# Split of the next image and close of the image before emitted in turn, in half-size pieces, with all planes made by GpSimd

## The chip, the cores and the metric

The kernel runs on one core of one Trainium2 chip. The metric is the device time of one execution in microseconds. A core has five engines that each run their own instructions in order: PE (matrix products), DVE (vector), ACT (scalar, activations), POOL (GpSimd) and SP (here it only issues DMAs). All work is in float32, but for some rows of the scan.

## What is computed

The input is x of shape (4, 96, 128, 128). Each of the four images goes through a state-space block (a projection, a depthwise convolution, four scans over the image, a layer norm, a projection back, added to x) and then through an attention block. The change lies in the second, cut here to what matters. `n` is the image after the first block, normalised; `sc`, `nc`, `res` are scalars of the input.

```
x   = n - mean(n)                                    # per image
x1  = relu(x);  x2 = x - x1                          # the split: positive and negative half
x1n = sqrt(pos/total) * layer_norm(x1 + avg1 * (x1 == 0))
x2n = sqrt(neg/total) * layer_norm(x2 + avg2 * (x1 > 0))
e   = 0.5 * (nc1*x1n + nc2*x2n) + res * x
x1, x2 = sc1*x1 + x1n, sc2*x2 + x2n

key, value = conv3x3(x1, aw1), conv3x3(x1, aw3)      # 96 -> 96 channels each
query, c2  = conv3x3(x2, aw2), conv3x3(x2, w_conv2)
attn = softmax(key . query over 3x3 patches / sqrt(96*9))    # a 96 x 96 x 3 x 3 kernel per image
o    = conv3x3(value, attn)
out  = x + e + w_full . [norm(o), x1 * norm(c2)] + b_full    # the close
```

## The kernel before, in words

**Stages.** Up to 2300 us the first block runs for all images. Then come four attentions, one image b after the other. The convolutions of images 1 to 3 are made from products of *planes*: a row of 128 pixels is cut into 32 groups of four, and six planes of 32 columns are linear combinations of neighbouring pixels. The planes of a half-image are made in SBUF, stored to DRAM (`x1p`, `x2p` for the two halves of the split, `vp` for the value) and read back by the attention in strips of 12 rows (`ya`, `yc`). Image 0 uses plain maps for its first convolutions and planes for the last one.

**Per image beside the attention**, a lighter stream of work runs:
- `norm` (`ssm_output`, L924) ends the first block and writes `xnew` to DRAM.
- `split_norm` (L1081) reads `xnew` twice. The first pass counts (L1123 to L1137). Then some forty small operations turn the sums into scales (L1142 to L1203). The second pass (L1222 to L1253) reads pieces of 8 rows (`SN` = 1024 elements per channel). ACT scales a half into PSUM (`bank`, L1243, two instructions of 512), DVE cuts it by the sign into `half` (L1247), and `planes_of` (L1372) makes the planes.
- `planes_of` has two ways. `scaled` (L1408), for the positive half: ACT makes two scaled copies, `x4` (L1411) and `x2` (L1412), and then POOL does ten additions and subtractions (L1420 to L1425 and four at L1390). `at_once` (L1392), for the negative half: DVE does nine operations (L1397 to L1404 and four at L1390) into `plv`. The caller's argument `vector=lambda i, second: second` picks the way. The value planes of the attention use `scaled` too.
- `close` (`attn_output`, L2247) of the image before reads `od`, `c2d` and `xnew` in pieces of 1024. ACT scales twice (L2231, L2236), DVE does four operations with two SBUF inputs (L2232, L2273, L2237, L2238), PE two matmuls per 512 (L2281, L2282), and DVE adds (L2284 for image 0, L2286 for the others). A memset on POOL (L2226) writes the row of ones into each piece of `o` before it is loaded.

**Order.** Each stream is a generator that emits instructions and yields a cost. `co_run` (L291) steps the attention, and for each cost that it yields steps the light stream until as much (times a pace) has been emitted. At the start of the next image the rest is emitted at once (`drain`, L2548). The light stream is a chain: norm, then split of image b+1, then close of image b-1 (L2552 to L2556). `until` (L2430) steps it further if the loads of the next image would read rows whose planes are not yet stored. `Later` (L306) holds pieces of work for a number of ticks. Engines then run in order, mostly by emission: a ready instruction may stand ahead of one that isn't, as at 4750 us, where PE runs products of image 2 between the matmuls of the close of image 0.

**Buffers** that the prediction speaks of: `x4` two, `x2` one, `pl` and `plv` one each, two tiles for the positive half and one for the negative (L1216), three for `xn`, and two banks of PSUM for the whole light stream (`psr`, L2509).

Of the kernel before, what the change touches and what calls it, by code (L numbers as in the profile page):

```python
# [69 lines left out]
def kernel(  # L70
# [273 lines left out]
    def chain(*gens):  # L344
        for g in gens:
            yield from g

# [733 lines left out]
    def split_norm(xnew, x1d, x2d, stats, keep, cnt, ps, side, planes, vector, done):  # L1081


        with ExitStack() as pools:
            p4 = pools.enter_context(tc.tile_pool(name="n4", bufs=3, side=side))
# [35 lines left out]
            p1 = ExitStack()  # L1121
            p2 = p1.enter_context(tc.tile_pool(name="n1", bufs=2, side=side))
# [15 lines left out]
            p1.close()  # L1138
            p2 = pools.enter_context(tc.tile_pool(name="n2", bufs=2, side=side))
            for i in range(3):  # L1140
                piece(i)
            c5 = col("c5", 5)  # L1142
            nc.vector.tensor_reduce(c5, cnt, AX.X, ALU.add)
            pt = bank(ps)[:C, 0:5]
            nc.tensor.matmul(pt, lhsT=mean96, rhs=c5, start=True, stop=True)
            g5 = col("g5", 5)
            nc.vector.tensor_scalar(g5, pt, float(C), None, ALU.mult)

            num, s1, s2 = col("num", 2), col("s1", 2), col("s2", 2)
            for d, at, of in ((num, 0, None), (s1, 1, 3), (s2, 2, 4)):  # L1150
                nc.vector.tensor_copy(d[:, 0:1], g5[:, at : at + 1])
                if of is None:
                    nc.vector.tensor_scalar(
                        d[:, 1:2], g5[:, 0:1], -1.0, TOTAL, ALU.mult, ALU.add
                    )
                else:
                    nc.vector.tensor_sub(d[:, 1:2], g5[:, of : of + 1], g5[:, at : at + 1])
            inv = col("inv", 2)
            nc.vector.reciprocal(inv, num)
            avg, navg = col("avg", 2), col("navg", 2)  # L1160
            nc.vector.tensor_mul(avg, s1, inv)
            nc.vector.tensor_scalar(navg, avg, -1.0, None, ALU.mult)

            var = col("var", 2)
            nc.vector.tensor_mul(var, s1, avg)
            nc.vector.tensor_sub(var, s2, var)
            nc.vector.tensor_scalar(var, var, 1.0 / TOTAL, 0.0, ALU.mult, ALU.max)


            sa = col("a", 2)  # L1170
            rsqrt2 = col("rsqrt2", 2)
            nc.vector.tensor_scalar(rsqrt2, var, LN_EPS, None, ALU.add)
            nc.scalar.activation(rsqrt2, rsqrt2, AF.Sqrt)
            nc.vector.reciprocal(rsqrt2, rsqrt2)
            nc.vector.tensor_scalar(sa, num, 1.0 / TOTAL, None, ALU.mult)
            nc.scalar.activation(sa, sa, AF.Sqrt)
            nc.vector.tensor_mul(sa, sa, rsqrt2)
            kept = col("kept", 9, 3)
            shift = kept[:, 0:2]
            nc.vector.tensor_mul(shift, sa, navg)  # L1180
            scale = kept[:, 2:4]
            nc.vector.tensor_add(scale, sa, scal[:, 0:2])


            rs, rh, half = col("rs", 2), col("rh", 2), col("half", 2)
            nc.vector.tensor_scalar(half, scal[:, 3:5], 0.5, None, ALU.mult)
            nc.vector.tensor_mul(rs, half, sa)
            nc.vector.tensor_mul(rh, half, shift)
            nc.vector.tensor_scalar(rs, rs, res, None, ALU.add)
            up, low = kept[:, 4:6], kept[:, 6:8]  # L1190
            nc.vector.tensor_sub(up[:, 0:1], rs[:, 0:1], rs[:, 1:2])
            nc.vector.tensor_sub(up[:, 1:2], rh[:, 0:1], rh[:, 1:2])
            nc.vector.tensor_copy(low[:, 0:1], rs[:, 1:2])
            nc.vector.tensor_add(low[:, 1:2], rh[:, 1:2], bful)

            for m, s in ((scale, shift), (up[:, 0:1], up[:, 1:2]), (low[:, 0:1], low[:, 1:2])):
                nc.vector.scalar_tensor_tensor(s, m, shift0, s, ALU.mult, ALU.add)
                nc.vector.tensor_scalar(m, m, a, None, ALU.mult)
            nc.vector.tensor_scalar(low[:, 0:1], low[:, 0:1], 1.0, None, ALU.add)
            thr = kept[:, 8:9]  # L1200
            nc.vector.reciprocal(thr, a)
            nc.vector.scalar_tensor_tensor(thr, shift0, -1.0, thr, ALU.mult, ALU.mult)
            keep.update(up=up, low=low, thr=thr, scale=scale, shift=shift)  # L1203

            def stored(i, m, h):
                if planes:
                    def then(pl):
                        store_planes(nc.sync, m, i * RS, RS, pl)
                        done[m is x2d] = (i + 1) * RS

                    return planes_of(later, p2, h, RS, then, vector=vector(i, m is x2d))
                at = (i * RS + 1) * PW
                return lambda: nc.scalar.dma_start(m[:, at : at + RS * PW], h)

            half = [
                [p2.tile([C, RS * PP], F32, name=f"half{j}{k}", bufs=1) for k in range(2 - j)]  # L1216
                for j in range(2)
                if planes
            ]
            for h in sum(half, []):  # L1220
                nc.gpsimd.memset(h.rearrange("p (a b) -> p a b", b=PB)[:, :, TN:PB], 0.0)
            for i in range(NS):  # L1222
                y = ahead.pop(0)
                piece(i + 3)
                for side_, m in ((0, x1d), (1, x2d)):
                    op = ALU.is_le if side_ else ALU.is_gt
                    if planes:
                        h = half[side_][i % len(half[side_])]
                        v, to = (
                            t.rearrange("p (a b) -> p a b", b=b)[:, :, 0:TN]  # L1230
                            for t, b in ((y, TN), (h, PB))
                        )
                        k, parts = TW * R, 2
                    else:
                        h = p2.tile([C, RS * PW], F32, name=f"half{side_}", bufs=4)
                        hv = h.rearrange("p (h w) -> p h w", w=PW)
                        nc.gpsimd.memset(hv[:, :, 0:1], 0.0)
                        v, to = y.rearrange("p (h w) -> p h w", w=W), hv[:, :, 1:PW]
                        k, parts = RS, 1
                    for a in range(0, k * parts, k):  # L1240
                        x, o = v[:, a : a + k], to[:, a : a + k]
                        f = part(ps, C, k, TN) if planes else o
                        nc.scalar.activation(  # L1243
                            f, x, AF.Identity,
                            scale=scale[:, side_ : side_ + 1], bias=shift[:, side_ : side_ + 1],
                        )
                        later(lambda o=o, x=x, f=f, op=op: nc.vector.scalar_tensor_tensor(  # L1247
                            o, x, thr, f, op, ALU.mult
                        ))
                    later(stored(i, m, h), 1 + 3 * side_ * planes)  # L1250
                for _ in range(6 if planes else 1):
                    later.tick()
                    yield 2.5 if planes else 3.5  # L1253
            later.flush()
# [117 lines left out]
    def planes_of(later, pool, t, r, then, most=RS, vector=False, bufs=2, p=C):  # L1372
# [19 lines left out]
        def at_once():  # L1392
            f = pool.tile([p, most, 6 * TN + 4], F32, name="diff", bufs=1)[:, :r]
            mid, outer, df = f[:, :, : 2 * PB], f[:, :, 2 * PB : 130], f[:, :, 130:]
            pl, to = planes("plv", 1)
            stt = nc.vector.scalar_tensor_tensor
            stt(mid, v[:, :, : 2 * PB], -a2, v[:, :, 2 * PB :], ALU.mult, ALU.add)  # L1397
            stt(
                outer, v[:, :, 2 * PB : 2 * PB + 2 * TN], -a2, v[:, :, 1 : 1 + 2 * TN],
                ALU.mult, ALU.add,  # L1400
            )
            nc.vector.tensor_sub(df, v[:, :, 2 * PB :], v[:, :, : 2 * PB])
            for i, f in ((3, AA), (4, -AA)):
                stt(to[i], df[:, :, 0:TN], f, df[:, :, PB : PB + TN], ALU.mult, ALU.add)  # L1404
            sums(nc.vector, mid, outer, to)
            later(lambda: then(pl))
# [840 lines left out]
    def attn_output(img, ps, side, share):  # L2247
        ob = out[img.b].rearrange("c h w -> c (h w)")
        with (
# [17 lines left out]
            for t in range(NS):  # L2267
                o, c2, xx = ahead
                if t + 1 < NS:
                    ahead = loads(t + 1)  # L2270
# [373 lines left out]
```

## Time and profile before

| what | value |
|---|---|
| time, median of 3 runs | 6557.2 us (6554.5 to 6562.6) |
| time of the profiled execution | 6572.0 us |
| its span, first to last instruction | 6570.2 us |
| granted TensorE clock, mean | 0.884 |
| PE, DVE, ACT, POOL busy over the span | 82%, 75%, 58%, 54% |
| attentions of images 0 to 3 (first products to last statistics) | 3698 to 3869, 3909 to 4743, 4858 to 5754, 5815 to 6525 us |
| splits of images 1, 2, 3 (second pass) | 3589 to 3912, 4290 to 4631, 5192 to 5541 us |
| closes of images 0, 1, 2 (first to last output piece) | 4680 to 4829, 5560 to 5755, 5780 to 6040 us |

The shares of the whole span mix stages with different limits, so the table of stretches is read first: it has one row per stretch, the busy time of each engine with the number of its instructions, the granted PE clock, the share of time that the DMA engines were busy, and GB/s. A line of waits reads: waiting engine and instruction, arrow, what it waited for; then microseconds in total, number of times, longest. A line of groups reads: source line, engine, operation, written tile, arrow, read tiles, shapes, count; then busy time, mean nanoseconds of one, and the idle time of the engine just before, with what ended it.

### The profile page before, as it was taken

The page shows a single profiled execution, that of the slowest core. Times are in us where ns is not written, and L with a number is a line of the kernel's source. Part 1 is how long each engine was busy: PE and PEld are TensorE (multiplying, and loading weights), DVE is VectorE, ACT ScalarE, POOL GpSimd, SP SyncE. Part 2 cuts the span into 40 slices and gives each one's busy share as a digit, 9 for nine tenths or more (in the row PEclk, how much of TensorE's full clock was granted, in tenths as well). Part 3 has the DMA queues.
Part 4 walks back from the last instruction along what each step waited for, and adds up shares of the span by engine and source line. Part 5 has one row for each costly group of instructions (what it writes and reads, how often), then busy time and mean ns, then how long its engine had stood idle before and what let it go on. Part 6 is the DMA issues. An engine that isn't in the chain of part 4 may idle for free. (4 is left out here: it accounts for less than half of the span.)

```text
span 6570.2 us, 76328 instructions
## 1 busy us (share of the span) xinstructions
PE 5365.0 (82%) x23264; PEld 2348.1 (36%) x23264; DVE 4934.7 (75%) x7469; ACT 3806.4 (58%) x4757; POOL 3533.2 (54%) x2744
## 2 busy tenths in 40 slices
PE   6889988987887835999987588876979777888888
PEld 2333323322222112444433244444424454344553
DVE  3247778988898768989745884687865788887867
ACT  1247768777787676677524464565544664444542
POOL 2236758978788546979522454466134574043430
PEclk9999989998998657999998799877988887998899
DMA  6767777776766757665676776655776555865658
GB/s 162 175 155 189 193 208 195 217 204 163 217 184 172 215 157 228 202 201 173 201 188 167 194 198 176 168 140 145 211 194 165 144 158 153 225 164 146 182 149 217
DMA packets 888486, 1198.29 MB, mean 182 GB/s; under 512 B 216142, under 2 KB 741014, under 8 KB 875596
## 3 DMA queue, kind: packets, MB, share of 16 engines
q1 hardware_dynamic: 864460, 1138.46, 63.7%
q0 software_dynamic: 16208, 38.42, 2.2%
q10 hardware_dynamic: 7408, 16.53, 0.8%
q8 instruction: 187, 3.06, 0.2%
q14 instruction: 223, 1.83, 0.1%
HBM read 777.62 MB, written 345.58 MB: 171 GB/s over the span
## 5 line engine op out<-in xcount | busy, mean ns | idle before, releaser
L622 PE MATMUL bank<-y,wp 128*128 128x512 f32 (+3 forms) x3584 | 1317.3, 626 | 86.3 <-DMA y<-y 33.8
L855 POOL TENSOR_TENSOR y<-y,dl 128x1024 f32<-128x1024 f32 x384 | 1058.0, 2755 | 271.8 <-DVE dl L847 252.6
L822 POOL TENSOR_TENSOR dl<-dl,u 128x1024 f32<-128x1024 f32 x384 | 1011.7, 2635 | 248.8 <-ACT dA L798 124.2
L843 DVE TENSOR_TENSOR_SCAN dA<-dA,pBC 128x512 f32<-128x512 f32 x768 | 981.4, 1278 | 30.7
L1488 PE MATMUL two<-ya,wd 128*64 128x192 f32 (+3 forms) x2376 | 600.6, 433 | 216.1 <-ACT odd L1559 106.8
L622 PEld LDWEIGHTS bank<-y,wp 128*128 128x128 f32 (+3 forms) x3584 | 459.0, 169 | 757.6 <-issue 656.0
L2119 PE MATMUL bank<-y,wn 128*128 128x384 f32 (+5 forms) x2408 | 678.0, 508 | 60.6 <-DMA y<-x1d 28.1
L847 DVE TENSOR_TENSOR dl<-dA,pBC 128x512 f32<-128x512 f32 x768 | 528.1, 688 | 257.6 <-PE pBC L736 185.0
L736 PE MATMUL pBC<-xr,wbc 60*128 60x512 bf16 (+1 forms) x1536 | 463.0, 405 | 316.4 <-DVE dA L843 245.3
L1922 ACT COPY yb<-ya 64x768 f32<-64x768 f32 (+1 forms) x660 | 537.9, 815 | 185.5 <-PE two L1488 122.1
L665 ACT ACTIVATE dl<-pd,dtb 128x512 f32<-128x512 f32 x768 | 486.2, 684 | 190.6 <-PE pd L736 175.2
L1488 PE MATMUL two<-yb,wd 128*64 128x192 f32 (+3 forms) x2376 | 573.3, 416 | 0.0
L826 DVE TENSOR_TENSOR pBC<-dl,pBC 128x512 f32<-128x512 f32 x768 | 527.6, 687 | 8.3 <-POOL dl L822 7.4
L2119 PEld LDWEIGHTS bank<-y,wn 128*128 128x128 f32 (+3 forms) x2408 | 310.7, 169 | 357.7 <-issue 194.1
L1488 PEld LDWEIGHTS two<-ya,wd 128*64 128x64 f32 (+1 forms) x2376 | 269.9, 174 | 433.3 <-ACT odd L1559 116.4
L798 ACT ACTIVATE dA<-dl,negA 128x1024 f32<-128x1024 f32 x384 | 420.3, 1141 | 2.3
L2226 POOL MEMSET o<- 1x1024 f32 x60 | 56.5, 949 | 602.8 <-PE bank L2281 296.0
L1992 POOL COPY own<-ring 32x512 f32<-32x512 f32 (+1 forms) x198 | 227.3, 1184 | 278.8 <-DVE ring L1581 237.1
L736 PEld LDWEIGHTS <-wbc 60*128 60x128 bf16 (+1 forms) x1536 | 103.2, 96 | 765.0 <-issue 752.0
L665 ACT ACT_TABLE_LOAD x248 | 318.2, 1283 | 97.4 <-PE pd L736 83.6
L1488 PEld LDWEIGHTS two<-yb,wd 128*64 128x64 f32 (+1 forms) x2376 | 298.2, 176 | 149.0 <-issue 41.1
L1002 PE MATMUL bank<-y,outws 96*96 96x512 f32 x512 | 298.3, 717 | 5.5 <-DVE r L1017 2.7
(323 smaller groups left out, 9888.6 us busy)
## 6 DMA issues: line engine op xcount, KB each, us to landing
u<-zb SPq DMA_DIRECT2D x192, 1024.0 KB
yms<-y SPq DMA_DIRECT2D x96, 512.0 KB
y<-yms SPq DMA_DIRECT2D x64, 768.0 KB
xn<-xnew SPq DMA_DIRECT2D x128, 384.0 KB
ya<-vp SPq DMA_DIRECT2D x120, 336.0 KB
y<-y SPq DMA_DIRECT2D x128, 258.2 KB
zb<-z SPq DMA_DIRECT2D x64, 512.0 KB
ya<-x1p SPq DMA_DIRECT2D x90, 336.0 KB
```

Of the source, the lines that this page charges most:

```text
L622: nc.tensor.matmul(blocks(pz[p:e]), lhsT=ws[k][:, d, c : c + e - p], rhs=window(ys[k], at, d, n), start=(i == 0), stop=(i == len(terms) - 1),)
L665: nc.scalar.activation(dst, src, AF.Softplus, bias=bias)
L736: nc.tensor.matmul(p, lhsT=w[rows], rhs=xr[rows, at : at + CH], start=True, stop=True)
L798: nc.scalar.activation(live[m]["dA"], live[m]["dl"], AF.Exp, scale=negA[:, g % 3, k : k + 1])
L822: nc.gpsimd.tensor_mul(t, t, u_view(n))
L826: nc.vector.tensor_mul(p, live[n]["dl"][:, bass.ts(half, CH)], p)
L843: nc.vector.tensor_tensor_scan(h, h, p, init, ALU.mult, ALU.add)
L847: nc.vector.tensor_mul(live[n]["dl"][:, sl], live[n]["dA"][:, sl], live[n]["C", half])
L855: nc.gpsimd.tensor_add(v, v, t.rearrange("p (a b) -> p a b", b=W))
L1488: nc.tensor.matmul(of(to[p:e], r), lhsT=w[:, i, c : c + e - p], rhs=tiles(t[k][PAIR[i]][:, SLOT[i]], o, r), start=(k == 0), stop=False,)
L1922: nc.scalar.copy(yb[k][64 * h - 64 : 64 * h, :, :n], ya[k][0:64, :, h * TN : h * TN + n])
L2119: nc.tensor.matmul(pc[p:e, :n].rearrange("p (h w) -> p h w", w=W), lhsT=w[:, c : c + e - p], rhs=v[:, :, 0:W], start=(i == 0), stop=(i == ...
```

## The change

The second pass of the split and the close are emitted in turn, a step of one and then a step of the other, by a new generator `together`, in place of one after the other. The counting pass becomes a generator of its own (`split_count`), and the scales a function (`split_scales`); their instructions stay. Both streams work in pieces of 512 elements (4 rows) in place of 1024. `at_once` goes: the planes of both halves are made by ACT and POOL. `x4` gets three buffers, `x2` two and `pl` three for the split, and each half two tiles; the value planes keep one of each. The memsets of the row of ones are done once per close. The image's total of emission cost stays: a split piece yields three times 2.5 (32 pieces in place of 16 with six), a close piece three times 2.6/3. For image 1 the split has no close beside it, for image 2's close there is no split. Image 0's split, not made into planes, keeps its piece size.

```diff
+    def together(*makers):
+        with ExitStack() as pools:
+            gens = [make(pools) for make in makers]
+            while gens:
+                for g in list(gens):
+                    got = next(g, 0)
+                    if got == 0:
+                        gens.remove(g)
+                    else:
+                        yield got
...
+    def split_pieces(pools, xnew, x1d, x2d, keep, cnt, ps, side, planes, done):
+        rows = R if planes else RS
+        n = rows * W
+        p2 = pools.enter_context(tc.tile_pool(name="n2", bufs=3, side=side))
...
+        for i in range(3):
+            piece(i)
+        split_scales(keep, cnt, ps)
...
+                return planes_of(later, p2, h, rows, then, rows, bufs=(3, 2, 3), wait=1)
...
+        half = [
+            [p2.tile([C, rows * PP], F32, name=f"half{j}{k}", bufs=1) for k in range(2)]
+            for j in range(2)
+            if planes
+        ]
...
+            nc.scalar.activation(
+                f, x, AF.Identity, scale=scale[:, j : j + 1], bias=shift[:, j : j + 1]
+            )
+            later(lambda: nc.vector.scalar_tensor_tensor(o, x, thr, f, op, ALU.mult))
+            later(stored(i, m, h), 1)
+
+        for i in range(L // n):
+            y = ahead.pop(0)
+            piece(i + 3)
+            of_half(i, y, 0, x1d)
+            if planes:
+                later(lambda i=i, y=y: of_half(i, y, 1, x2d))
...
+            for _ in range(3 if planes else 1):
+                later.tick()
+                yield 2.5 if planes else 3.5
...
-    def planes_of(later, pool, t, r, then, most=RS, vector=False, bufs=2, p=C):
+    def planes_of(later, pool, t, r, then, most, bufs=(1, 1, 1), p=C, wait=2):
...
-        def at_once():
-            f = pool.tile([p, most, 6 * TN + 4], F32, name="diff", bufs=1)[:, :r]
...
-            sums(nc.vector, mid, outer, to)
-            later(lambda: then(pl))
...
-        return at_once if vector else scaled
+        return scaled
...
-            for t in range(NS):
...
-                first_half(img, xx, x1)
...
-                residual(img, xx, e)
-                for h in range(2):
...
+        with_one = [p1.tile([128, CH], F32, name=f"o{k}")[0 : C + 1] for k in range(2)]
+        for o in with_one:
+            nc.gpsimd.memset(o[C : C + 1], 1.0)
+        cost = 2.6 / 3 * share
...
+        for t in range(NCH):
+            o, c2, xx = ahead
+            x1, e = (p3.tile([C, CH], F32, name=n) for n in ("x1", "e"))
+            for y, m, s in ((x1, scale[:, 0:1], shift[:, 0:1]), (e, up[:, 0:1], up[:, 1:2])):
+                nc.scalar.activation(y, xx, AF.Identity, scale=m, bias=s)
+            yield cost
+            if summed:
+                added(*summed)
+            stt(x1, xx, thr, x1, ALU.is_gt, ALU.mult)
+            stt(c2, c2, s2[0:C, 0:1], x1, ALU.subtract, ALU.mult)
+            ahead = loads(t + 1)
+            yield cost
+            stt(e, xx, thr, e, ALU.is_gt, ALU.mult)
+            stt(e, xx, low[:, 0:1], e, ALU.mult, ALU.add)
+            pf = part(ps, C, CH)
+            nc.tensor.matmul(pf, lhsT=w1, rhs=o, start=True, stop=False)
+            nc.tensor.matmul(pf, lhsT=w2, rhs=c2, start=False, stop=True)
+            summed = t, pf, x1, e
+            yield cost
+        added(*summed)
...
-                after.append(imgs[b + 1].norm(yms[(b + 1) // 2][(b + 1) % 2], psr, "right"))
-                after.append(
-                    imgs[b + 1].split(psr, "right", lambda i, second: second)
-                )
-            after.append(imgs[b - 1].close(psr, "right", 1.0 if b + 1 < NB else 2.0))
+                after.append(new.norm(yms[(b + 1) // 2][(b + 1) % 2], psr, "right"))
+                after.append(new.count(psr, "right"))
+                beside.append(lambda pools, new=new: new.split(pools, psr, "right"))
+            beside.append(
+                lambda pools, old=imgs[b - 1], share=share: old.close(pools, psr, "right", share)
+            )
+            after.append(together(*beside))
```

## The prediction

> **What bounds the kernel now.** I read the busy time by stretch first, to find the stages that the change touches, then the waits in one of them, then the groups of instructions by shape. The change works in three places: S1, the split of image 1 (3590 to 3912 us); S2, the split of image 2 and the close of image 0 (4290 to 4830); S3, the split of image 3 and the close of image 1 (5195 to 5810). Lines L1243 and L2273 give these times.
>
> ```profile
> core 0: us, PE busy (x) PEld busy (x) DVE busy (x) ACT busy (x) POOL busy (x), PEclk, DMA share, GB/s
> 3590.00:3912.00 322.00, 205.29 (x801) 98.35 (x801) 289.99 (x552) 172.97 (x235) 161.76 (x209) 0.81 0.72 193
> 4290.00:4602.00 312.00, 225.88 (x1393) 144.19 (x1392) 256.87 (x471) 177.71 (x245) 213.83 (x274) 0.79 0.52 140
> 4602.00:4830.00 228.00, 195.93 (x655) 80.29 (x656) 193.07 (x281) 110.67 (x127) 32.17 (x35) 0.92 0.77 215
> 5195.00:5527.00 332.00, 252.78 (x1684) 166.09 (x1680) 288.63 (x491) 193.93 (x266) 252.72 (x316) 0.83 0.52 140
> 5527.00:5810.00 283.00, 242.27 (x842) 103.56 (x843) 237.97 (x338) 132.92 (x156) 35.70 (x40) 0.92 0.74 202
> ```
>
> Rows 1, 2 and 4 are split stretches. DVE is busiest (90, 82 and 87%), PE falls to 64, 72 and 76%, POOL has 50, 69 and 76%. Rows 3 and 5 are close stretches: PE and DVE share the load, POOL has 14 and 13%. So the split is short of DVE, the close leaves POOL idle, and they stand one behind the other. The waits of the second split stretch of S3 show how a late POOL or DVE reaches PE:
>
> ```profile
> ACT x L1412 <- POOL pl L1425: 34.2, 14, 7.5
> PEld two L1488 <- ACT odd L1559: 34.2, 6, 9.1
> PE two L1488 <- ACT odd L1559: 33.2, 6, 8.9
> ACT bank L1243 <- DVE half L1247: 25.9, 15, 4.9
> ACT x L1411 <- POOL pl L1390: 21.6, 6, 5.1
> ```
>
> ACT runs in order. It stands for x4 and x2 to be read by POOL (56 us) and for DVE (26 us), and behind it wait the copies `odd` and `ends`, for which PE waits 33 us. The same chain decides what the change does.
>
> **Price of the planes.** The rows of one split stretch (4290 to 4602) by shape; the small shapes are the value planes of the last strip, which have just the element counts of a 4-row piece (264, 256, 128):
>
> ```profile
> L1390 POOL TENSOR_TENSOR pl<-x 96x256 f32<-96x256 f32 x56 | 40.6, 737 | 0.0
> L1390 POOL TENSOR_TENSOR pl<-x 128x128 f32<-128x128 f32 x8 | 3.8, 497 | 0.0
> L1420 POOL TENSOR_TENSOR x<-own,x 128x264 f32<-128x264 f32 x2 | 1.3, 654 | 0.0
> L1421 POOL TENSOR_TENSOR x<-own,x 128x256 f32<-128x256 f32 x2 | 1.3, 638 | 0.0
> L1390 DVE TENSOR_TENSOR plv<-diff 96x256 f32<-96x256 f32 x56 | 44.2, 830 | 0.0
> L1404 DVE SCALAR_TENSOR_TENSOR plv<-diff 96x256 f32<-96x256 f32 x28 | 19.4, 711 | 8.0 <-DMA x2p<-plv 7.9
> ```
>
> On POOL now: 1169 (L1420) + 1284 (L1421) + 655 (L1422) + 811 (L1423) + 724 + 754 (L1424, L1425) + 4x737 = 8345 ns for 8 rows of a half, x16 = 134 us per image. After: 64 pieces of 4 rows. Each is 654 + 638 + 646 + 456 + 433 + 433 + 4x497 = 5248 ns by the small rows. Only two instructions stand behind the 646; with 433 it is 5035. Exact halving would give 4172. I take 5.0 us: 320 us per image, bounds 267 and 336. POOL also loses the 16 memsets of a close (L2226, 949 ns each): -15.
>
> DVE loses 863 + 956 + 941 + 2x711 + 4x830 = 7502 ns x16 = 120 us per image. For three images that is 360 off DVE and 3x(320 - 134) = 558 onto POOL, less 45.
>
> ACT gains the second half's scalings: 64x(653 for 528 elements + 431 for 264) less 16x(1073 + 654) = +42. The close in halves costs ACT 772 (L1243, 512 elements) x2 against 1238 (L2231): +10 at most. On DVE its four operations with two SBUF inputs cost 5425 ns per 1024 now (1342, 1328, 1388, 1367). A 512 lies between half of that and 697 + (1342 - 697)/3 = 912, on the line from a hindered 256-element row (L1404): 0 to +30 us per image. I take +15, because POOL will be busy beside them.
>
> [...]
>
> **What is hidden.** Plane stores and loads double in number: per image 32 more stores, 16 more loads of `xn`, 48 more loads and 16 more stores of the close, 112 issues on SP's queue. At 0.56 us (an `x1p` store) that is 63 us in some 550, on a queue whose instructions take 110 of the 332 us of the S3 split; bytes stay. I cost it at nothing; if its cover goes, the `ya` loads of the strips come late. The more buffers (x4 3, x2 2, pl 3) remove POOL's wait for plane stores (86 us before L1422 in all). Image 0's split keeps its sizes: nothing. The close of image 2 stands alone: +15 DVE and +10 ACT at most, against memsets that held up POOL; I take 0 (bounds -8 and +15).
>
> **Sum by stage.** Work after, by the terms above (us):
> S1, 322 long: POOL 162 - 134 + 320 = 348; DVE 170; ACT 215; PE 205.
> S2, 540: POOL 246 - 134 - 15 + 320 = 417; DVE 450 - 120 + 15 = 345; ACT 340; PE 422.
> S3, 615: POOL 288 - 149 + 320 = 459; DVE 422; ACT 379; PE 495.
>
> The emission costs say where it lands. A strip pair costs 38.6, all strips with the weights 425, the last convolution 79. Norm and count take 188, a round of split and close 10.1, 32 rounds 323. So some 73% of the rounds of S3 fall into the strips (425 - 188 = 237), 67% of S2's (about 20 are still taken by split 1), the rest beside the last convolution. The engine that binds can be filled to between 0.88 (DVE, 163 of 186 us beside the close of image 1) and 0.95 (DVE, 103 of 108 at 3590 to 3698).
>
> S3, strips: POOL 253 - 134 + 0.73x320 = 353 in 332. At 0.95 that is 371, +39. But the strips need their own planes only a strip later (54 us), so some of it can slide into the next stretch; bound then PE, 253 + some 37 for the close's matmuls, at 0.88 330: 0. I take +10. Behind it: PE 242 - 37 = 205 and no more a DVE bound, 231 at 0.89 against 283, -52; unless POOL's rest is in the way. I take -35. Together -25.
> S2, strips: 214 - 117 + 0.67x320 = 311, at 0.95 327, +15; slid on, -15; I take 0. Behind it (228 us, of which 86 a drain that only the close's DVE chain sets): 182 to 195, -35. Together -35.
> S1 has no close beside it. POOL 348 at 0.95 is 366, +44. If a strip's 54 us slide into the norm of image 2 (POOL 127 of 273), 309, -13. Taken +15.
> All: +15 - 35 - 25 + 0 = -45 us. The profiled execution is 6572.0 (span 6570.2 and 1.8 around), so 6527. The median of the runs shown lies 15 lower, 6557.2: 6512, rounded 6515.
>
> **Rivals.**
> POOL takes DVE's place (slower). Nothing slides, since ACT stands at x4 and x2, and DVE at `half`, which POOL still reads; behind ACT stand `odd` and `ends`, and PE for them. Place: strips of S2 and S3, all of S1. At 0.95 +44 - 20 + 4 = +28; at 0.88 S1 395, strips 353 and 401: +73 + 6 + 34 = +113. Middle +70: 6627. It decides once POOL needs more than about 0.9 of a stretch. For it: 348 of 322 and 353 of 332. Against: 54 us of room per strip, and the attention of image 0 uses no POOL.
> The load spreads evenly. S1 -13, S2 422/0.9 = 469, -71, S3 495/0.9 = 550, -65: -149, 6408. For it: no engine is above 0.83 of S2 and S3. Against: the costs put 73% into the strips.
> Gains and losses cancel, within 0.2% (13 us, about what a measurement of this kernel can tell from none): 6557. For it: the terms have both signs.
>
> **Chances.** Forecast (-100 to -13) 0.38, even spread 0.14, no change 0.12, POOL as the bound 0.36. Hence faster 0.52, same 0.12, slower 0.36. The forecast's own range is 6457 to 6544; with the rivals on both sides 6430 to 6640 leaves out about 2 in 10.
>
> **What would show it.** Right: POOL at some 960 us (3x320) for the split planes, about 5.0 us for a piece of 4 rows of one half; POOL's share in the close stretches from 14% to above 40%; no drain after the last convolution of image 1; attention 2 starting earlier. Wrong: ACT's waits for POOL in the strips above 100 us, strips of S2 or S3 longer than 350 us, or a 4-row piece far from 5.0 us. A piece above 5.6 us would make the slower case the likely one.

## The result

| | before | after |
|---|---|---|
| time, median of 4 runs | 6557.1 us (6554.5 to 6562.6) | 6657.1 us (6653.9 to 6662.8) |
| ratio, with 95% interval | 1 | 1.0152 (1.0135 to 1.0170) |
| span of the profiled execution | 6570.2 us | 6656.4 us |
| PE, DVE, ACT, POOL busy | 5365, 4935, 3806, 3533 us | 5402, 4809, 3932, 3963 us |

The change costs 100 us. The forecast was a gain of 45 us (6515), so the sign was wrong. 6657 lies on the side of the slower rival, beyond its middle of 6627, within its +28 to +113, and outside the stated range. Work did move as the diff says: DVE has 126 us less, POOL 430 us more.

**Where the time went.** Each stage ends with a named instruction of the trace, so stages of different kernels can be set side by side: the end of a counting pass, the start of the softmax's exponentials (the end of the strips), the last output of an attention, the last addition of a close, the last statistics of a norm.

| us | before | after | difference |
|---|---|---|---|
| S1: end of count 1 to end of norm 2 | 636.5 | 684.8 | +48 |
| S2: strips of image 1 | 277.6 | 305.6 | +28 |
| S2: behind them, to the end of close 0 | 264.7 | 251.2 | -14 |
| norm and count of image 3 | 357.1 | 374.9 | +18 |
| S3: strips of image 2 | 336.4 | 395.7 | +59 |
| S3: behind them | 231.3 | 192.6 | -39 |
| image 3 to the end | 816.3 | 823.2 | +7 |

The rest (all up to count 1, and count 2) differs by -22 us, and the change doesn't touch the first block: over the fourteen kernels profiled here the end of count 1 lies anywhere between 3558 (the changed kernel) and 3586 us. The stretches behind the strips became shorter, as forecast. The strips became longer.

The stretches of the changed kernel follow: split 1; strips of S2 and behind them; strips of S3 and behind them. The columns are those of the table of stretches before.

```profile
core 0: us, PE busy (x) PEld busy (x) DVE busy (x) ACT busy (x) POOL busy (x), PEclk, DMA share, GB/s
3566.00:3940.00 374.00, 233.04 (x920) 112.78 (x919) 245.26 (x438) 216.09 (x338) 305.51 (x667) 0.79 0.64 172
4323.00:4673.00 350.00, 268.71 (x1462) 155.91 (x1461) 251.79 (x396) 194.28 (x302) 280.61 (x522) 0.79 0.51 145
4673.00:4870.00 197.00, 165.91 (x563) 69.35 (x561) 147.32 (x224) 125.40 (x186) 114.61 (x237) 0.88 0.69 196
5245.00:5641.00 396.00, 310.62 (x1829) 186.95 (x1827) 300.12 (x478) 224.53 (x348) 309.19 (x578) 0.84 0.49 141
5641.00:5833.00 192.00, 157.78 (x541) 67.33 (x541) 144.28 (x231) 124.26 (x181) 104.95 (x227) 0.89 0.75 213
```

The reader should look for a full engine and find none. POOL has 82, 80 and 78% of the three split stretches (lines 1, 2 and 4 below the heading); the slower rival expected it at 88 to 95%. In line 4 PE and POOL stand equal at 78%, DVE at 76%. So the strips are not simply short of POOL: engines wait for one another. The waits in the strips of S3 (5245 to 5641 us) say where:

```profile
ACT x L1431 <- POOL pl L1444: 55.7, 21, 6.4
PEld bank L2320 <- DVE c L2313: 34.3, 13, 9.1
...
PEld two L1507 <- ACT odd L1578: 29.7, 7, 9.9
PE two L1507 <- ACT odd L1578: 28.4, 7, 9.8
PE bank L2320 <- DVE c L2313: 28.0, 10, 8.5
```

ACT's wait for x2 is there (the first line). New are the two lines with `c` (the second and the last): PE and its weight loads, inside the strips, wait for the close's `c` on DVE, up to 9 us at a time. The groups of the three later images (3560 to 6360 us) by shape name the instruction that is late:

```profile
L1425 POOL TENSOR_TENSOR pl<-x 96x128 f32<-96x128 f32 x768 | 344.4, 459 | 0.0
...
L2312 DVE SCALAR_TENSOR_TENSOR x<-xx,kept,x 96x512 f32<-96x512 f32 x96 | 150.5, 1567 | 69.4 <-ACT x L2308 63.4 <-DMA out<-x 5.4
...
L1439 POOL TENSOR_TENSOR x<-half,x 96x264 f32<-96x264 f32 x192 | 131.8, 686 | 180.9 <-ACT x L1430 170.3 <-DVE sm L1686 9.7
...
L1440 POOL TENSOR_TENSOR x<-half,x 96x256 f32<-96x256 f32 x192 | 129.3, 673 | 0.1
L2320 PE MATMUL bank<-c,w 96*96 96x512 f32 x192 | 125.2, 739 | 110.8 <-DVE c L2313 109.7 <-DMA xx<-xnew 0.5
...
L1442 POOL TENSOR_TENSOR x<-x 96x128 f32<-96x128 f32 x192 | 93.2, 485 | 74.9 <-ACT x L1431 74.6
L1443 POOL TENSOR_TENSOR pl<-pl,x 96x128 f32<-96x128 f32 x192 | 92.0, 479 | 0.1
...
L1441 POOL TENSOR_TENSOR pl<-half 96x128 f32<-96x128 f32 x192 | 88.1, 459 | 61.0 <-DMA x2p<-pl 34.0 <-DVE half L1275 22.3 <-DMA x1p<-pl 3.4
L1444 POOL TENSOR_TENSOR pl<-pl,x 96x128 f32<-96x128 f32 x192 | 87.6, 456 | 0.1
L2317 DVE SCALAR_TENSOR_TENSOR e<-xx,kept,e 96x512 f32<-96x512 f32 x96 | 86.1, 897 | 0.1
L2316 DVE SCALAR_TENSOR_TENSOR e<-xx,kept,e 96x512 f32<-96x512 f32 x96 | 86.0, 896 | 0.1
L2313 DVE SCALAR_TENSOR_TENSOR c<-c,s,x 96x512 f32<-96x512 f32 x96 | 84.5, 880 | 0.1
L1431 ACT ACTIVATE x<-half 96x264 f32<-96x264 f32 x192 | 81.6, 425 | 198.5 <-POOL pl L1444 198.2
```

The four DVE lines (L2312, L2313, L2316, L2317) are the close's operations with two SBUF inputs. L2312 takes 1567 ns, 1.7 times the others, with the same shape. A mean hides how: of its 96 executions the middle one takes 748 ns, and eleven take 78 of the 150 us. PE's matmul on `c` (L2320) then waits 110 us for DVE in all. The same two groups of the kernel before, whose first operation works on pieces of 1024:

```profile
L2282 PE MATMUL bank<-c,w 96*96 96x512 f32 x192 | 110.6, 706 | 34.2 <-DVE c L2273 33.8
...
L2232 DVE SCALAR_TENSOR_TENSOR x<-xx,kept,x 96x1024 f32<-96x1024 f32 x64 | 85.9, 1342 | 63.7 <-ACT x L2231 63.6
```

There PE waited 33.8 us. The longest of the eleven, in the timeline of the strips of S3, of which the lines of DVE and some of POOL are shown (start and duration in us, engine, line, operation, and the idle time before it):

```profile
5358.86 11.02 DVE L2312 SCALAR_TENSOR_TENSOR x<-xx,kept,x 96x512 f32<-96x512 f32 x1 [4.13 <-ACT x L2308]
5358.93 0.88 POOL L1440 TENSOR_TENSOR x<-own,x 128x384 f32<-128x384 f32 x1
...
5359.75 0.48 POOL L1442 TENSOR_TENSOR x<-x 96x128 f32<-96x128 f32 x1
...
5368.48 0.46 POOL L1425 TENSOR_TENSOR pl<-x 96x128 f32<-96x128 f32 x1
5368.89 0.44 POOL L1443 TENSOR_TENSOR pl<-pl,x 96x128 f32<-96x128 f32 x1
5369.80 0.74 DVE L2316 SCALAR_TENSOR_TENSOR e<-xx,kept,e 96x512 f32<-96x512 f32 x1
```

The wait for ACT is over and the profile counts the instruction as running, yet it doesn't end until POOL, after 22 additions and subtractions without a pause, stops at 5369.33; 0.55 us later DVE is done. It stands, not for a semaphore, but for as long as POOL has work back to back. The next operation, with POOL idle, takes 0.74 us. All eleven began while a POOL instruction was running. Eight of them ended 0.55 us after POOL's run of instructions did; the other three ended 0.55 to 0.64 us after an instruction of POOL, with the next one begun.

From this come two theories for the 100 us. **C (collision)**: emitted in turn, the close's DVE operations stand beside POOL's planes, POOL holds them up, and PE and everything behind DVE wait. **P (POOL's load)**: POOL has 430 us more to do, and its chain with ACT over x4 and x2 sets the pace, as in the rival. Two more were open: **T**, that emitting in turn is itself harmful, and **S**, that the smaller pieces are. The expectations, put down before each run, use more letters: S there is the close's and D the split's small pieces, and Q is the waiting for POOL's queue wherever the close's operations stand.

### The profile page after: what moved, and what is told of

It is laid out like the page before. It is cut to its first block, busy times and chain, and to the rows that moved or that the text cites. A ratio compares the mean times of both kernels' runs of the same rounds, so it can differ in the third digit from the quotient of the medians.

```text
span 6656.4 us, 78702 instructions
## 1 busy us (share of the span) xinstructions
PE 5402.4 (81%) x23264; PEld 2361.0 (35%) x23264; DVE 4808.8 (72%) x7229; ACT 3931.9 (59%) x5141; POOL 3963.2 (60%) x4145
## 5 line engine op out<-in xcount | busy, mean ns | idle before, releaser
L1425 POOL TENSOR_TENSOR pl<-x 96x128 f32<-96x128 f32 (+1 forms) x1032 | 496.7, 494 | 0.0
L1507 PE MATMUL two<-ya,wa 128*96 128x384 f32 (+1 forms) x528 | 235.2, 530 | 111.0 <-DMA ya<-vp 57.5
```

The costliest lines, as they stand in the source:

```text
L1425: op(to[i], x, y)
L1507: nc.tensor.matmul(of(to[p:e], r), lhsT=w[:, i, c : c + e - p], rhs=tiles(t[k][PAIR[i]][:, SLOT[i]], o, r), start=(k == 0), stop=False,)
```

## The experiments

Each ratio is to the kernel before, run on the same chip beside it, with its 95% interval; 1% is 66 us. The kernel before itself scatters by some 50 us within such a set of runs (one execution of 12217 us, beside e5 to e8, is not counted), so differences below 10 us are not read. Line numbers differ a little from kernel to kernel.

### Take the change apart: who makes the planes, and in which order

The first four part the planes from the order: e1 and e3 put back one of the two each, e4 both, and e2 puts the planes alone into the kernel before. **e1**: the changed kernel, the second half's planes on DVE again, in pieces of 4 rows; to make room `x4` and `pl` have two buffers in place of three.

```diff
-                return planes_of(later, p2, h, rows, then, rows, bufs=(3, 2, 3), wait=1)
+                return planes_of(later, p2, h, rows, then, rows, bufs=(2, 2, 2), wait=1, vector=m is x2d)
...
-        return scaled
+        return at_once if vector else scaled
```

> The changed kernel with the second half's planes made by DVE again (nine operations for 4 rows); in turn and half-size stay, x4 and pl get two buffers instead of three to make room. Theory P (POOL's added work, 558 us of it, delays ACT, DVE and PE): the loss of 100 us goes, 6560 or less, since the close beside the last convolution is already 39 us shorter. Theory T (the close in the strips stops PE, which waits there for DVE at its matmuls, 62 us in the strips of images 1 and 2): stays above 6620, and the strips of image 2 (387 us from count to softmax after, 336 before) above 370.

**e2**: the kernel before, with all planes on POOL.

```diff
-                    imgs[b + 1].split(psr, "right", lambda i, second: second)
+                    imgs[b + 1].split(psr, "right", lambda i, second: False)
```

> The kernel before, with the second half's planes made by ACT and POOL too; pieces of 8 rows, one buffer each for x2 and pl, split and close one after the other. P: slower by 80 us or more (6640 or more), and all of it in the splits, where POOL needs 134 us more in 312 to 336. T: 6557 within 20.

**e3**: the changed kernel, with split and close one after the other again.

```diff
-            after.append(together(*beside))
+            after += [together(make) for make in beside]
```

> The changed kernel with split and close one after the other again, all else as changed. P: at least as slow as the changed kernel, 6650 to 6720, with POOL above 0.9 in the strips of images 1 and 2 beside the split. T: the loss goes, 6570 or less, and PE's waits for DVE at the close's matmuls go from the strips.

**e4**: both edits, those of e1 and e3. What remains of the change are the pieces of half the size.

> Half-size pieces, the scales function and the early memsets alone: second half on DVE, one after the other. P and T: 6557 within 25. [...]

| ratio to before | planes of the second half on DVE | all on POOL |
|---|---|---|
| one after the other, pieces as before | 1 | e2: 1.0181 (1.0134 to 1.0228) |
| one after the other, half-size pieces | e4: 1.0085 (1.0052 to 1.0118) | e3: 1.0307 (1.0275 to 1.0338) |
| in turn, half-size pieces | e1: 0.9981 (0.9963 to 0.9998) | after: 1.0152 (1.0135 to 1.0170) |

The median times are 6562.2 us (e1), 6680.0 (e2), 6773.1 (e3) and 6629.6 (e4), with 6576.9 for the kernel before among them. Read along a row, the move to POOL costs 1.7 to 2.2% whatever the order (112 us in turn; in the lower two rows the third buffers of `x4` and `pl` go with it). Read down a column, emitting in turn gains 1.0% with DVE and 1.6% with POOL: T falls. Half-size pieces cost 0.85% with the planes on DVE and 1.3% with them on POOL. So, taken through the left column, the 1.52% of the change is +0.85 - 1.04 + 1.71: the one part that was meant to relieve DVE loses more than the change does. Two results lie outside what was expected: e3 lost more than its 6650 to 6720, and e4, at 6629.6, lies above its 6557 within 25.

In e3 the rival's mechanism shows almost pure. First its stretch of the strips of S3, then the group of ACT's x2 over the three images:

```profile
5294.00:5682.00 388.00, 257.17 (x1722) 167.60 (x1720) 185.12 (x372) 222.25 (x353) 351.88 (x727) 0.81 0.43 118
```

```profile
L1431 ACT ACTIVATE x<-half 96x264 f32<-96x264 f32 x192 | 82.3, 428 | 274.9 <-POOL pl L1444 274.4
```

POOL is busy 351.9 of 388 us, 91%, DVE 48%. The prediction put 353 us of POOL work into these strips, at a fill of 0.88 to 0.95 for 371 to 401 us. Hardly any collision is in it: the operation that took 1567 ns takes 796 in e3, since the close stands behind the split. In the changed kernel the strips hold less of POOL (309 us) and are still longer. Another cause must be at work there, and C names it.

### Take the collision away

**e5**: the changed kernel, the close's four operations made with one SBUF input.

```diff
+        def one_input(to, x):
+            nc.vector.tensor_scalar(to, x, 0.0, None, ALU.is_gt, ALU.add, accum_out=junk)
...
-            stt(x1, xx, thr, x1, ALU.is_gt, ALU.mult)
-            stt(c2, c2, s2[0:C, 0:1], x1, ALU.subtract, ALU.mult)
+            one_input(x1, x1)
+            one_input(c2, x1)
...
-            stt(e, xx, thr, e, ALU.is_gt, ALU.mult)
-            stt(e, xx, low[:, 0:1], e, ALU.mult, ALU.add)
+            one_input(e, e)
+            one_input(e, e)
```

> The changed kernel, where the close's four DVE operations per piece with two SBUF inputs are replaced by one-input operations with an accumulator, of about the same length (0.6 us and 0.08 for the accumulator, against 0.73 unhindered); its output isn't the reference's. Theory C (the loss comes from DVE standing at these operations while POOL works: they take 880 to 1567 ns on average in the changed kernel, some 150 us in all above the unhindered): 6600 or less. Theory Q (the loss comes from ACT and DVE waiting until POOL has read x4, x2 and half, wherever the close's operations stand): no more gained than by the same replacement beside DVE-made planes, 25 us, 6630 or more.

**e6**: the control, the same edit on e1, where POOL is not so full.

> The control: the same replacement in the version in turn with the second half on DVE. C and Q: 6562 less 10 to 30 us (423 us of these operations against some 350).

e5 takes 6549.9 us, a ratio of 0.9968 (0.9949 to 0.9988), 1.84% below the changed kernel, some 121 us. e6 takes 6507.6, 0.9893 (0.9868 to 0.9918), 0.88% below e1, some 58 us. The group of the first operation in e5:

```profile
L2297 DVE TENSOR_SCALAR_CACHE_REDUCE x<-x 96x512 f32<-96x512 f32 x96 | 65.3, 680 | 79.1 <-ACT x L2311 78.8
```

680 ns, and 79 for reading the accumulator, where it was 1567. The strips of S2 and S3 take 274 and 345 us, against 306 and 396. So C holds. The control fell by more than was expected of it: DVE's operations are held up beside a half-loaded POOL as well (the four take 852 to 885 ns in the mean in e1, where the middle one of the changed kernel takes 742 to 748). And e5 stays 0.75% above e6, so POOL's load costs something without any collision.

e5 changes what is computed, and its operations no longer read `c2` and `xx`. The same can be had with the close's sums unchanged: ACT writes the scaled copy into a bank of PSUM, and DVE then has one input in SBUF and one in PSUM. **e9** is this on e1, **e10** on the changed kernel.

```diff
-            for y, m, s in ((x1, scale[:, 0:1], shift[:, 0:1]), (e, up[:, 0:1], up[:, 1:2])):
-                nc.scalar.activation(y, xx, AF.Identity, scale=m, bias=s)
+            f = part(ps, C, CH)
+            nc.scalar.activation(f, xx, AF.Identity, scale=scale[:, 0:1], bias=shift[:, 0:1])
...
-            stt(x1, xx, thr, x1, ALU.is_gt, ALU.mult)
-            stt(c2, c2, s2[0:C, 0:1], x1, ALU.subtract, ALU.mult)
+            stt(f, xx, thr, f, ALU.is_gt, ALU.mult)
+            stt(c2, c2, s2[0:C, 0:1], f, ALU.subtract, ALU.mult)
...
+            f = part(ps, C, CH)
+            nc.scalar.activation(f, xx, AF.Identity, scale=up[:, 0:1], bias=up[:, 1:2])
...
-            stt(e, xx, thr, e, ALU.is_gt, ALU.mult)
-            stt(e, xx, low[:, 0:1], e, ALU.mult, ALU.add)
+            stt(f, xx, thr, f, ALU.is_gt, ALU.mult)
+            stt(e, xx, low[:, 0:1], f, ALU.mult, ALU.add)
```

> In turn, second half on DVE, and the close's two scaled copies written by ACT into PSUM and cut there by DVE, so that none of its four DVE operations has two SBUF inputs; the result is the reference's. Theory C (collisions of the close's operations with POOL): near the control with one-input operations, 6508: 6500 to 6530, below both kernels. If the two PSUM banks of the light stream, now shared by two more users per piece, hold ACT up: above 6560.

> The changed kernel with the same close over PSUM, all planes still on POOL. C: the 107 us that the one-input operations gained come back, 6550 to 6575. Q (waits for POOL's queue alone): 6630 or more.

e10 takes 6542.1 us, 0.9966 (0.9949 to 0.9983): with this one edit the change gains 0.3% where it lost 1.5%. e9 takes 6510.9, 0.9910 (0.9879 to 0.9940), and beats both kernels. In e10 the groups of the close on DVE, and ACT's wait for x2:

```profile
L1431 ACT ACTIVATE x<-half 96x264 f32<-96x264 f32 x192 | 81.1, 422 | 128.0 <-POOL pl L1444 127.6
...
L2312 DVE SCALAR_TENSOR_TENSOR bank<-xx,kept,bank 96x512 f32<-96x512 f32 x96 | 71.9, 749 | 105.7 <-ACT bank L2308 98.8 <-DMA ya<-vp 2.4 <-DMA yc<-vp 2.0
L2318 DVE SCALAR_TENSOR_TENSOR bank<-xx,kept,bank 96x512 f32<-96x512 f32 x96 | 71.9, 748 | 1.8 <-ACT bank L2316 1.5
...
L2313 DVE SCALAR_TENSOR_TENSOR c<-c,s,bank 96x512 f32<-96x512 f32 x96 | 70.7, 737 | 0.3
L2319 DVE SCALAR_TENSOR_TENSOR e<-xx,kept,bank 96x512 f32<-96x512 f32 x96 | 70.7, 736 | 0.5
```

All four are at 736 to 749 ns, beside the same additions on POOL. That is no less than the middle L2312 of the changed kernel took (748), so the operations are not faster by themselves; the long ones are gone. They took 407 us and now take 285, and the kernel's time falls by about the same 120 us. In e9 they take 284 us where e1 has 334, and the time falls by 0.7%, again about as much. (The edit also moves ACT's second scaling a step later; e5, which leaves ACT alone, gains the same.) ACT's wait for x2 falls too, from 198 to 128 us, though not in S1 (72 in both): where DVE stood, `half` and the strips' own work came late to POOL as well, which is read from the trace and was not tested by itself. By stages, with e1 and e9 for comparison:

| us | before | after | e10 | e1 | e9 |
|---|---|---|---|---|---|
| S1 | 636.5 | 684.8 | 691.0 | 648.9 | 651.6 |
| S2: strips | 277.6 | 305.6 | 277.6 | 288.5 | 294.4 |
| S2: behind them | 264.7 | 251.2 | 219.5 | 230.7 | 226.2 |
| norm and count of image 3 | 357.1 | 374.9 | 382.2 | 368.4 | 358.2 |
| S3: strips | 336.4 | 395.7 | 349.6 | 372.2 | 352.9 |
| S3: behind them | 231.3 | 192.6 | 187.4 | 185.4 | 181.4 |
| image 3 to the end | 816.3 | 823.2 | 799.2 | 815.8 | 802.4 |

The reader is to see two things. In S2 and S3 e10 wins back 28 and 46 us of strips with POOL's load unchanged. In S1, where no close runs, e10 wins nothing back: 691 us like the changed kernel, 39 above e9. That is P. Over the whole kernel e10 is 0.56% above e9, so of the 1.71% that the move to POOL costs in turn about a third is left without the collision.

### The size of the pieces

**e7**: the kernel before, with only its close replaced by that of the changed kernel: pieces of 512, the addition one piece later, the next loads behind the first two operations.

```diff
-            for t in range(NS):
-                o, c2, xx = ahead
-                if t + 1 < NS:
-                    ahead = loads(t + 1)
...
+        for t in range(NCH):
+            o, c2, xx = ahead
...
+            stt(c2, c2, s2[0:C, 0:1], x1, ALU.subtract, ALU.mult)
+            ahead = loads(t + 1)
+            yield cost
```

> The kernel before with the close of the changed kernel (pieces of 512, memsets once) and nothing else. The half-size version one after the other was 53 us slower than before, and its drain after the attention of image 1 took 127 us instead of 86. Theory S (the small close pieces are the cost: two more DVE operations and one more load round trip per 512): 6600 or more, drain above 115 us. Theory D (the small split pieces are: DVE 458 us for its planes against 341): 6570 or less.

**e11**: e7 with the loads two pieces ahead, and three buffers for them.

```diff
-        with_one = [p1.tile([128, CH], F32, name=f"o{k}")[0 : C + 1] for k in range(2)]
+        with_one = [p1.tile([128, CH], F32, name=f"o{k}")[0 : C + 1] for k in range(3)]
...
-                y = p3.tile([C, CH], F32, name=name)
+                y = p3.tile([C, CH], F32, name=name, bufs=3)
...
-        ahead = loads(0)
+        ahead = [loads(0), loads(1)]
...
-            ahead = loads(t + 1)
+            ahead.append(loads(t + 2))
```

> The kernel before with the small close, whose loads now run two pieces ahead (three buffers) instead of one. If the small close lost its 45 us to waiting for loads: back to 6575 or less, drain after the attention of image 1 below 100 us (129 with one ahead, 86 with pieces of 1024). If to the number of its operations and the chain from ACT over DVE and PE back to DVE in each piece: 6600 or more, drain above 115.

e7 takes 6609.6 us, 1.0062 (1.0041 to 1.0083): the new close alone costs 41 us, and e4's 0.85% adds little to it that the intervals can tell. The rest of close 0 behind the attention grows from 86 to 129 us. e11 takes 6586.3, 1.0021 (1.0003 to 1.0038), with 116 us there. About two thirds of the cost are gone with earlier loads (or with the buffers that go with them, which this run doesn't separate); the rest stays open, and both the time and the 116 us lie between the two cases expected. In the changed kernel this stretch is 54 us, since the close in turn is mostly done by then.

### Share the planes out

Would a smaller part on POOL be better than all or half? **e8**: e1 with every fourth piece of the second half on POOL. **e12**: the same on e9.

```diff
-                return planes_of(later, p2, h, rows, then, rows, bufs=(2, 2, 2), wait=1, vector=m is x2d)
+                return planes_of(later, p2, h, rows, then, rows, bufs=(2, 2, 2), wait=1, vector=m is x2d and i % 4 < 3)
```

> In turn, second half on DVE but every fourth piece of it on POOL. If time follows the share of the planes on POOL evenly: 6562 + 95/4 = 6586. If POOL's load only costs beyond a threshold, or DVE is the one that is short: 6565 or less.

> As the first of these, with every fourth piece of the second half on POOL. With the collisions of the close gone POOL's load should be cheaper: 6490 to 6520 if DVE (0.93 busy in the strips of image 2 with the half on it) is still what binds; 6520 to 6545 if time goes evenly with the share on POOL (42 us for all of it between the two one-input versions).

e8 takes 6564.4 us, 0.9989 (0.9971 to 1.0008), no different from e1. e12 takes 6549.6, 0.9967 (0.9952 to 0.9983): not better than e9 but 0.57% worse, almost at e10's level. That was not expected, and a quarter of the move costing as much as all of it doesn't fit a cost in proportion to POOL's load. The trace of e12 has its profiled execution at 6531 us, below its median, so its stages don't show the loss. It stays open.

## Why the prediction was wrong

**The step that failed** is the price of the close's operations beside POOL: "A 512 lies between half of that and 697 + (1342 - 697)/3 = 912, on the line from a hindered 256-element row (L1404): 0 to +30 us per image. I take +15, because POOL will be busy beside them." Measured: 407 us for the three images against 260 before (48 pieces x 5425 ns), +49 per image, above the upper bound. Three operations keep to it (880 to 897 ns); L2312 breaks it with 1567. For the small size alone +15 was right: e7 has 803 + 783 + 768 + 767 = 3121 ns x32 = 100 against 87 per image, +13. The other 36 is the collision, and the bound came from the mean of a row hindered at POOL's old load, which doesn't tell how long an engine waits beside one that doesn't pause: the longest L2312 stood 11.0 us, through 22 instructions of POOL. With one input in SBUF and one in PSUM the first operation takes 749 ns in e10, where it took 1567.

**The sum took it as work on an engine with room.** DVE did have room: 300 of 396 us in the strips of S3, standing time counted in, and 252 of 350 in e10 without it. But DVE runs in order: while the eleven long L2312 stood, 78 us in all, it began nothing else until their last 0.1 us. Behind them wait the additions on the products of the strips, `c` for PE, and `half` for POOL. So 36 us per image (107 in three, 122 against e10) became about 120 us in time (e5, e10): next to nothing of it was hidden. The prediction priced the two parts of the change apart; that the turn-taking puts the close exactly beside the planes that the other part makes long, it had only as the +15. In e3 and e4, one after the other, the same operations take 762 to 801 ns.

**S1: "Taken +15"** was the second miss. It came to +48, the end without sliding (+44). e10 has +54 there, so the collision isn't in it. POOL fills only 82% of split 1, 306 of 374 us. The waits of that stretch (3566 to 3940 us) show where the other 68 go: 37 are POOL's waits for ACT's copies x4 and x2, 25 a single wait for a plane store, 7 for DVE's `half`. ACT in turn waits 97 us for POOL to read x4 and x2, and DVE 79 us for POOL to read `half`. So the engines hand each piece to and fro. This is the rival's mechanism, at a lower fill than it had; it is read from the waits, while e10 against e9 shows only that the move to POOL is what costs the time. "If a strip's 54 us slide into the norm" didn't happen: norm 2 took 374 us against 350.

**S2 and S3** would have been nearly right without the collision. Strips: taken 0 and +10, measured +28 and +59, in e10 0 and +13. Behind: taken -35 and -35, measured -14 and -39, in e10 -45 and -44. The load that the forecast let slide does slide out of the strips when DVE is not held up, and DVE's relief does shorten what follows. But norm and count of image 3, which nothing was charged for, take 18 us more (25 in e10, but 1 in e9, with those planes on DVE): what slides falls there.

**POOL's price** was right: a piece of 4 rows takes 686 + 673 + 459 + 485 + 479 + 456 + 4x459 = 5074 ns (5.0 predicted), 974 us for the three images (960 predicted). Set end to end this is a little too much: the instructions overlap by some 40 ns in the trace, and POOL's busy time with them is 906 us. That is most of why POOL's busy time rose by 430 us and not by the 513 of the sum (558 less 45). "The more buffers (x4 3, x2 2, pl 3) remove POOL's wait for plane stores" was half right: 37 of 86 us are left (L1441). Its wait for the stores of the value planes, which kept one buffer, rose from 59 to 120 us; it is 136 us in e9, the second fastest of all these kernels, so it doesn't decide. The doubled number of transfers, "at nothing" in the sum, is not the main cause either, since e9 and e10 have it too and are faster than the kernel before.

**What was to show it.** POOL's share behind the strips rose to 58 and 55% (above 40% predicted). The drain after image 1 shrank from 86 to 54 us, but did not go. Attention 2 started at 4936 us against 4858, later and not earlier. The sign "strips of S2 or S3 longer than 350 us" came true with 396 in S3. The sign "ACT's waits for POOL in the strips above 100 us" did not: 72 us in the strips of S3 (55.7 of them the x2 shown), against 56. It was a sign of the rival alone, and the strips were long for another reason.

**The rivals.** "POOL takes DVE's place" had the direction, and the right price for S1 (+44 at a fill of 0.95, measured +48) and for the strips of S3 in e3 (371 to 401, measured 388); e2 lost 119 us, just above its +113. In the changed kernel as it stands POOL fills no stretch beyond 82%, against the 0.88 to 0.95 that this rival reckoned with, and taking away the collision takes away the whole loss, so it is not the main cause. The even spread fell with the strips, which hold the load more than before. The unpriced cost of the halved close (41 us by itself in e7, where the sum has it at +15 on DVE and +10 on ACT at most, and its loads "at nothing") is covered again by the turn-taking in e1, whose net is -0.2%.

## What to carry to other kernels

Before work is moved to POOL, or placed beside POOL's work, list DVE's instructions with two SBUF inputs that will run there, and ask whether POOL will have pauses; one such instruction at the head of DVE's queue cost up to fifteen times its length here (11.0 us for one of 0.72), and everything behind it waited too. Having ACT write one of the two operands into PSUM took that away here for no more instructions, and gained 0.7% with the planes on DVE and 1.9% with them on POOL. And when a change has two parts, price the pair: what one part makes long, the other may put beside its worst neighbour.

## What the runs showed of the hardware that was not expected

A DVE operation with two SBUF inputs was held up here not by one POOL instruction but by a whole run of them. The 0.72 us operation stood 11.0 us through 22 additions of POOL, and ended 0.55 us after the last. Eleven of 96 stood for over 3 us, while the middle one took 748 ns; of the other three operations one in 288 did. In e1, where POOL has half of the split's planes to make, the same operation takes 874 ns in the mean, against 1567. So a mean of such a group says little; the longest one and what POOL does beside it say more.

POOL's additions on their side were hardly slowed in the mean: 459 ns (L1425, 128 elements) in the changed kernel, 442 in e10 without the collision. But it goes the other way too, and the trace of the kernel before already had it. In S1 there DVE also makes planes of image 0, and a POOL subtraction of which the middle one takes 642 ns stood for 10.03 us, through 36 DVE operations without a pause, most of them with two SBUF inputs. It ended 0.5 us after the last of these. Two lines of the timeline of the kernel before:

```profile
3647.40 10.03 POOL L1422 TENSOR_TENSOR pl<-half 96x256 f32<-96x256 f32 x1
...
3656.44 0.47 DVE L1454 SCALAR_TENSOR_TENSOR pl<-diff 96x128 f32<-96x128 f32 x2
```

So in these two places the engine that worked back to back held up the other, whichever it was: DVE stood 11.0 us, POOL 10.03 us.
